# Sending the last four tiles' rows from the sync engine in a gated cross-attention and ternary FFN block, with another order of the end

## The chip, the cores and the metric

The kernel runs on one core of a Trainium2 chip. Its time is device microseconds of one execution; the median of several executions is given. The engines are named as in the profile: PE (TensorE), DVE (VectorE), ACT (ScalarE), POOL (GpSimd) and SP (the sync engine, which here only starts transfers).

## What is computed

For 16 batches of 224 rows of 512 numbers, a Flamingo-like block: attention of the normalised rows to a masked context, added to the rows with a gate, and then a feed-forward layer whose weights are rounded to -1, 0 or 1 and whose activations are rounded to 8 bits, added with a second gate. Cut to what matters here:

```python
def act_quant(x):
    scale = 127.0 / clip(max(abs(x), axis=-1), 1e-05)
    return clip(round(x * scale), -128.0, 127.0) / scale

def bitlinear(x, w, b):                     # w: ternary after weight_quant
    return einsum('bsd,fd->bsf', act_quant(rmsnorm(x)), weight_quant(w)) + b

def ffn(x, w1, b1, w2, b2):                 # 512 -> 2048 -> 512
    return bitlinear(gelu(bitlinear(x, w1, b1)), w2, b2)

x = x + tanh(g_xattn) * attention(layernorm(x), ctx, mask)
x = x + tanh(g_ffn) * ffn(layernorm(x), w1, b1, w2, b2)
```

## The kernel before

**Order of the rows.** The masks leave a different number of context rows in each batch, so the kernel sorts the batches by that number and treats them in that order. The 3584 rows make 28 tiles of 128 rows; seven tiles hold four batches, so a tile can hold the end of one batch and the start of the next. The table `sh.token` holds for each place in a tile the number of its row in memory, computed on the chip. Rows are fetched (`fetch_x`) and the results sent (`store`) by indirect transfers that POOL starts and that read their row numbers from this table.

**Pairs.** The feed-forward part treats the tiles in 14 pairs (`NPAIR`); tile (i, k) is tile 2i + k. A tile goes through `residual` (fetch), `project` (the attention's output projection, added on DVE at line 1255), `normalise` (the rounding to 8 bits; the result `xq` is turned by a transposing transfer from SP, or, in the last pair, by PE in `turn_rows`), `up` (w1 on PE, eviction to `h` on DVE), `gelu`, `down` (w2 on PE) and `store`.

`gelu` applies the function on ACT, takes the largest absolute value on DVE (line 1369), scales to 16-bit integers in the tile `hq` (line 1372), casts these to bf16 (line 1375 on DVE; line 1379 in two halves on ACT for pair 12), and has `hq` turned into `hqT`: by a transposing transfer from SP, or for tile (12, 1) by PE in `turn_by_tensor`, whose result ACT copies (line 1355). ACT also sums the squares, and POOL makes of them and of the maximum the factor `c2` (lines 1272 to 1274).

**The last pair** has its own functions, since nothing lies behind it to fill the engines. `up_last` works in halves of 1024 columns: eviction (DVE, line 1419), gelu (ACT, line 1422), maximum of the half (DVE, line 1423). `gelu_last` takes the maximum of the two (line 1434), and scales and casts each half (lines 1441 and 1442). `mean_square` sums the squares on ACT, `measure_last` makes `c2` on POOL. `turn_by_tensor` turns `hq` on PE.

**Who orders the work.** The framework puts each engine's instructions in an order by the program's text and its own reckoning of what is ready, and adds the semaphores. `tc.issue_after(x)` asks that what is traced in its block stands behind `x` on the engine of `x`. Each engine then runs its instructions strictly in that order. At the end of the program, written out by hand, the calls are:

```python
    mean_square(i, 1)
    added, sent = store(i - 1, 1)
    gelu_last(i, 0)
    with tc.issue_after(added):
        gelu_last(i, 1)
    with tc.issue_after(raised):
        turn_by_tensor(i, 0)
    with tc.issue_after(sent):
        measure_last(i, 0)
        measured = measure_last(i, 1)
```

with i = 13. `store` adds the product to the rows on DVE (line 1485) and sends them from POOL (line 1487). The whole compact path stands in a branch on `n_odd` (line 250 loads it into every engine's registers); line 1826 is the end of the program, where SP waits for every transfer and each engine drains and meets the others.

Of the kernel before, what the change touches and what calls it, by code (L numbers as in the profile page):

```python
# [734 lines left out]
def compact_path(ctx, tc, sh, x, context, out, late_loads, stages):  # L735
# [541 lines left out]
    def normalise(i, ks=(0, 1)):  # L1277
        f = pairs[i]
        y = f["y"]
        name = f"{i}_{ks[0]}"  # L1280
        part = slice(ks[0], ks[-1] + 1)
        mv = small(f"mv_y{name}", 4).rearrange("p (k n) -> p k n", k=2)
        if ks[0] == 0:
            f["fx"] = late["rows"].tile([P, 2, D], F32, tag="hq", name=f"fx_{i}", bufs=3)
            f["xq"] = pa.tile([P, 2, D], BF16, tag="xq", name=f"xq_{i}", bufs=3)
            f["xqT"] = pa.tile([P, 2 * ND, P], BF16, tag="xq", name=f"xqT_{i}", bufs=3)
        fx, xq, xqT = f["fx"], f["xq"], f["xqT"]
        for k in ks:
            st = small(f"bs_y{name}_{k}", 6)
            nc.vector.bn_stats(st, y[:, k, :])  # L1290
            nc.vector.bn_aggr(mv[:, k, :], st)
            nc.vector.tensor_scalar(fx[:, k, :], y[:, k, :], mv[:, k, 0:1], None, ALU.subtract)  # L1292
        amax = small(f"a1_{name}")
        nc.vector.tensor_reduce(amax[:, part], fx[:, part, :], AX.X, ALU.max, apply_absolute_value=True)

        scale = quantiser(amax, part, 1e-5 * EPS, f"1_{name}")

        for k in ks:
            nc.vector.tensor_scalar(xq.bitcast(I16)[:, k, :], fx[:, k, :], scale[:, k : k + 1], None, ALU.mult)
        rounded = nc.vector.tensor_copy(xq[:, part, :], xq.bitcast(I16)[:, part, :])  # L1300
        if i < NPAIR - 1:
            nc.sync.dma_start_transpose(
                out=xqT[:, ks[0] * ND : (ks[-1] + 1) * ND, :], in_=xq[:, part, :].rearrange("p n d -> p (n d)")
            )

        r = small(f"r1_{name}")
        nc.gpsimd.tensor_scalar(r[:, part], mv[:, part, 1], 1.0 + EPS, EPS * EPS, ALU.mult, ALU.add)
        pow_half(r[:, part])
        c = unquantiser(amax, r, part, sh.isw[0], f"1_{name}")
        for k in ks:  # L1310
            f["c1", k] = c[:, k : k + 1]
            nc.gpsimd.tensor_tensor(y[:, k, :], y[:, k, :], sh.b2, ALU.add)  # L1312
        load["v"] += len(ks) * (850 + 340 + 667 + 450 + 220)
        return rounded.ins
# [43 lines left out]
    def gelu(i, ks=(0, 1)):  # L1358
        f = pairs[i]
        name = f"{i}_{ks[0]}"  # L1360
        part = slice(ks[0], ks[-1] + 1)
        ss = small(f"ss_{name}")
        amax = small(f"a2_{name}")
        for k in ks:
            if (i, k) != (NPAIR - 2, 1):
                nc.scalar.activation(f["h", k], f["h", k], AF.Gelu)  # L1366
        for k in ks:
            h = f["h", k]
            nc.vector.tensor_reduce(amax[:, k : k + 1], h, AX.X, ALU.max, apply_absolute_value=True)  # L1369
            scale = quantiser(amax, slice(k, k + 1), 1e-5 * EPS**0.5, f"2_{i}_{k}")  # L1370
            hq = late["rows"].tile([P, FF], BF16, tag="hq", name=f"hq_{i}_{k}", bufs=3)
            nc.vector.tensor_scalar(hq.bitcast(I16), h, scale[:, k : k + 1], None, ALU.mult)  # L1372
            f["hqT", k] = hqT = late["rows"].tile([P, NF, P], BF16, tag="hqT", name=f"hqT_{i}_{k}", bufs=2)
            if i < NPAIR - 2:
                late["rounded"] = nc.vector.tensor_copy(hq, hq.bitcast(I16)).ins
            else:
                for g in range(2):
                    cols = slice(g * FF // 2, (g + 1) * FF // 2)
                    nc.scalar.copy(hq[:, cols], hq.bitcast(I16)[:, cols])
            f["hq", k] = hq  # L1380
            if (i, k) != (NPAIR - 2, 1):
                nc.sync.dma_start_transpose(out=hqT, in_=hq)
        if (i, ks[0]) == (NPAIR - 2, 1):
            f["a2", 1] = amax[:, 1:2]
            return
        for k in ks:
            nc.scalar.activation(f["h", k], f["h", k], AF.Square, accum_out=ss[:, k : k + 1])  # L1387
        r = small(f"r2_{name}")
        nc.gpsimd.tensor_scalar(r[:, part], ss[:, part], 1.0 / FF, EPS, ALU.mult, ALU.add)
        pow_half(r[:, part])  # L1390
        c = unquantiser(amax, r, part, sh.isw[1], f"2_{name}")
        for k in ks:
            f["c2", k] = c[:, k : k + 1]
        load["v"] += len(ks) * (2282 + 1280 + 690)
        load["s"] += len(ks) * 2 * 1910 + 2600

    def up_last(i, k):

        f = pairs[i]
        if k == 0:  # L1400
            place = pa.tile([P, 12, S], F32, tag="pT", name="h_last", bufs=1)
            h = place.rearrange("p n q -> p (n q)")[:, :FF]
        else:
            h = xoT.rearrange("p n q -> p (n q)")[:, :FF]
        most = small(f"am_{i}_{k}")
        for g in range(2):
            ph = wide([P, 2, NB], F32, f"hp_{i}_{k}_{g}")
            for n in range(2):
                at = (2 * g + n) * NB
                for d in range(ND):  # L1410
                    last = nc.tensor.matmul(
                        ph[:, n, :],
                        lhsT=f["xqT"][:, k * ND + d, :],
                        rhs=w1T[:, d, at : at + NB],
                        start=(d == 0),
                        stop=(d == ND - 1),
                    )
            cols = slice(2 * g * NB, 2 * (g + 1) * NB)
            nc.vector.scalar_tensor_tensor(
                h[:, cols], ph.rearrange("t i n -> t (i n)"), f["c1", k], sh.b1[:, cols], ALU.mult, ALU.add  # L1420
            )
            nc.scalar.activation(h[:, cols], h[:, cols], AF.Gelu)
            nc.vector.tensor_reduce(most[:, g : g + 1], h[:, cols], AX.X, ALU.max, apply_absolute_value=True)
        f["h", k], f["most", k] = h, most
        return last.ins

    def gelu_last(i, k):

        f = pairs[i]
        name = f"{i}_{k}"  # L1430
        part = slice(k, k + 1)
        h = f["h", k]
        amax = small(f"a2_{name}")
        nc.vector.tensor_reduce(amax[:, part], f["most", k], AX.X, ALU.max)
        scale = quantiser(amax, part, 1e-5 * EPS**0.5, f"2_{name}")
        hq = late["rows"].tile([P, FF], BF16, tag="hq", name=f"hq_{name}", bufs=3)
        f["hqT", k] = hqT = late["rows"].tile([P, NF, P], BF16, tag="hqT", name=f"hqT_{name}", bufs=2)
        half = FF // 2
        for g in range(2):
            cols = slice(g * half, (g + 1) * half)  # L1440
            nc.vector.tensor_scalar(hq.bitcast(I16)[:, cols], h[:, cols], scale[:, part], None, ALU.mult)
            nc.vector.tensor_copy(hq[:, cols], hq.bitcast(I16)[:, cols])
        f["hq", k], f["a2", k] = hq, amax[:, part]

    def mean_square(i, k):
        f = pairs[i]
# [15 lines left out]
    def measure_last(i, k):  # L1462
        f = pairs[i]
        c = unquantiser(f["a2", k], f["r2", k], slice(0, 1), sh.isw[1], f"2_{i}_{k}")
        f["c2", k] = c[:, 0:1]
        return latest["p"]
# [14 lines left out]
    def store(i, k):  # L1481
        f = pairs[i]
        po = f["po", k]
        y = f["y"][:, k, :]
        added = nc.vector.scalar_tensor_tensor(y, po, f["c2", k], y, ALU.mult, ALU.add)  # L1485
        load["v"] += 700
        sent = nc.gpsimd.indirect_dma_start(  # L1487
            out=out_rows,
            out_offset=bass.IndirectOffsetOnAxis(ap=token(2 * i + k), axis=0),
            in_=y,  # L1490
            in_offset=None,
            bounds_check=B * S - 1,
            oob_is_err=False,
        )
        return added.ins, sent.ins

    NPAIR = NTOK // 2

# [212 lines left out]
    for s in range(B):  # L1711
# [33 lines left out]
        if s + 1 < B:  # L1745
            scores(s + 1, 0)
            scores(s + 1, 1)

    i = NPAIR - 1
    residual(i)  # L1750
    with tc.issue_after(late["av"]), tc.issue_after(late["rounded"]):
# [27 lines left out]
        turn_by_tensor(i - 1, 1)  # L1779
        lowered = down(i - 1, 1)  # L1780
    mean_square(i, 1)
    added, sent = store(i - 1, 1)
    gelu_last(i, 0)
    with tc.issue_after(added):
        gelu_last(i, 1)
    with tc.issue_after(raised):
        turn_by_tensor(i, 0)
    with tc.issue_after(sent):
        measure_last(i, 0)
        measured = measure_last(i, 1)  # L1790
    with tc.issue_after(lowered):
        down(i, 0, lambda: turn_by_tensor(i, 1))
    with tc.issue_after(measured):
        store(i, 0)
    down(i, 1)
    store(i, 1)

# [33 lines left out]
```

## Time and profile before

| | |
|---|---|
| median of 3 runs | 740.0 us (739.37 to 740.6) |
| the profiled execution: its time | 735.04 us |
| its span, first to last instruction | 733.0 us |
| mean granted PE clock | 0.981 |
| PE busy | 676.0 us (92%) |
| DVE busy | 492.2 us (67%) |
| ACT busy | 416.2 us (57%) |
| POOL busy | 394.1 us (54%) |
| indirect sends of results, POOL | 28 |
| transposing transfers, SP | 25 of `hq`, 14 of `xq` |

The profile is of one execution. Busy shares are over the whole span; the change concerns the last 60 us, so the shares say little of it, and the lines of that stretch are read instead. In lines of the timeline the first column is the start and the second the length, in us from the start of the span; in brackets stands how long the engine was idle before, and what ended this. "PEq", "SPq" and so on are an engine's sequencer, which waits, branches, drains or starts transfers. Lines of the source are those of the kernel before.

### The profile page before, as it was taken

The numbers are of one execution on the slowest core, as the hardware profiler recorded it, in microseconds if no ns is written. First come the engines' busy times: TensorE is split into PE (matmuls) and PEld (weight loads), VectorE is DVE, ScalarE is ACT, GpSimd is POOL, SyncE is SP. The second block draws the span as 40 slices with busy tenths as digits, with TensorE's granted clock in tenths as the row PEclk, the third lists the DMA queues.
The fourth block names the chain that finished last, engine by engine and source line by source line (L and its number), as shares of the span: only waits on it lengthen the run. The fifth ranks groups of instructions, "written<-read, shape, count | busy, mean of one in ns | idle before, by whom it ended". The sixth has DMA issues, their size and how long they took to land.

```text
span 733.0 us, 11422 instructions
## 1 busy us (share of the span) xinstructions
PE 676.0 (92%) x3917; PEld 432.1 (59%) x3917; DVE 492.2 (67%) x1294; ACT 416.2 (57%) x978; POOL 394.1 (54%) x549
## 2 busy tenths in 40 slices
PE   4998899999999999897999999999999999999862
PEld 3876677666555656564556665766665665544331
DVE  5586856877484775673667857839585765889760
ACT  2549555384673864646627549547373746574560
POOL 5583676464464644755447562656545453554631
PEclk9989999999999999999999999999999999999997
DMA  7884031032222232321233321123313221422200
GB/s 236 288 288 144 14 104 32 16 75 57 65 54 58 83 58 72 70 59 58 54 61 104 58 81 38 41 72 74 83 43 72 58 59 44 86 73 58 58 15 33
DMA packets 79858, 56.74 MB, mean 77 GB/s; under 512 B 68176, under 2 KB 68320, under 8 KB 79664
## 3 DMA queue, kind: packets, MB, share of 16 engines
q1 hardware_dynamic: 71728, 30.17, 17.6%
q0 software_dynamic: 8064, 25.76, 11.4%
q8 instruction: 33, 0.54, 0.3%
q14 instruction: 33, 0.27, 0.1%
HBM read 32.06 MB, written 7.34 MB: 54 GB/s over the span
## 4 chain that ended last, share of the span: by engine, by line
PE 63%; DVE 10%; issue 9%; POOL 9%; ACT 4%; DMA 3%; POOLq 0%; DVEq 0%; ACTq 0%
PE qp L1066 11%; PE op L1252 10%; PE fp L1472 8%; PE hp L1333 8%; PE kp L946 5%; PE sim L1106 4%; PE vp L962 4%; PE ptp L1163 3%; PE av L1188 2%; POOL p L1140 2%; DVE a L1369 2%; PE xnp L1045 2%; POOL x L808 2%; DMA hqT<-hq 1%; POOL out_dram L1487 1%
## 5 line engine op out<-in xcount | busy, mean ns | idle before, releaser
L1140 POOL TENSOR_TENSOR p<-p,rec 112x768 f32<-112x768 f32 (+2 forms) x64 | 79.6, 1246 | 72.0 <-DVE rec L1139 28.1
L1130 ACT ACTIVATE p<-p,nm 112x192 f32<-112x192 f32 (+2 forms) x256 | 104.8, 413 | 10.3 <-DVE nm L1120 7.3
L1472 PE MATMUL fp<-w2T,hqT 128*128 128x512 fp8e4 x448 | 102.6, 382 | 3.8 <-DMA hqT<-hq 2.2
L1066 PE MATMUL qp<-xnT,wq_sb 128*128 128x224 f32 x512 | 105.1, 359 | 0.6 <-ACT xnT L781 0.6
L1252 PE MATMUL op<-wo_sb,xoT 128*128 128x512 f32 x224 | 103.7, 599 | 0.0
L1333 PE MATMUL hp<-w1T,xqT 128*128 128x512 fp8e4 x416 | 99.3, 383 | 3.0 <-DVE nm L1120 1.4
L1066 PEld LDWEIGHTS qp<-xnT,wq_sb 128*128 128x128 f32 x512 | 97.0, 193 | 6.4 <-issue 3.1
L1341 DVE SCALAR_TENSOR_TENSOR h<-hp,c,b_bc 128x1024 f32<-128x1024 f32 x52 | 66.5, 1281 | 43.6 <-PE hp L1333 43.3
L1120 DVE CUSTOM_DVE_ANT_0 p<-sim,mask 112x192 f32<-112x192 f32 (+2 forms) x224 | 56.0, 303 | 32.5 <-PE sim L1106 31.9
L1472 PEld LDWEIGHTS <-hqT 128*128 128x128 bf16 x448 | 42.7, 98 | 58.8 <-issue 6.3
L1369 DVE TENSOR_REDUCE a<-h 128x1 f32<-128x2048 f32 x26 | 59.3, 2281 | 20.3 <-ACT h L1366 20.3
L1487 POOL DMA_INDIRECT out_dram<-y,token x28 | 32.0, 1143 | 67.2 <-DVE y L1485 62.1
L1333 PEld LDWEIGHTS <-xqT 128*128 128x128 bf16 x416 | 39.9, 98 | 47.4 <-issue 8.5
L1485 DVE SCALAR_TENSOR_TENSOR y<-fp,c,y 128x512 f32<-128x512 f32 x28 | 20.9, 746 | 68.0 <-PE fp L1472 66.4
L1252 PEld LDWEIGHTS op<-wo_sb,xoT 128*128 128x128 f32 x224 | 40.7, 190 | 38.8 <-issue 36.3
L946 PE MATMUL kp<-ctxT,wk_sb 128*128 128x192 f32 (+1 forms) x360 | 59.9, 316 | 0.0
L946 PEld LDWEIGHTS kp<-ctxT,wk_sb 128*128 128x128 f32 x360 | 54.5, 198 | 5.4 <-issue 3.8
L1387 ACT ACTIVATE h<-h 128x2048 f32<-128x2048 f32 x25 | 47.7, 1909 | 17.1 <-DVE hq L1372 11.8
L1312 POOL TENSOR_TENSOR y<-y,b_bc 128x512 f32<-128x512 f32 x28 | 37.0, 1321 | 34.6 <-DVE fx L1292 34.3
L781 ACT COPY pT<-ptp 128x448 f32<-128x448 f32 (+1 forms) x62 | 32.3, 536 | 39.9 <-PE ptp L1163 39.7
L781 ACT COPY qT<-qp 128x448 f32<-128x448 f32 x29 | 15.4, 532 | 65.7 <-PE qp L1066 65.4
L1106 PE MATMUL sim<-kT,qT 64*112 64x192 f32 (+2 forms) x512 | 50.8, 311 | 0.6 <-DVE nm L1120 0.6
(200 smaller groups left out, 1250.5 us busy)
## 6 DMA issues: line engine op xcount, KB each, us to landing
raw<-in_L_ffn_w_dram SPq DMA_DIRECT2D x16, 512.0 KB, 5.4
wq_sb<-in_L_xattn_W_q_dram SPq DMA_DIRECT2D x1, 1024.0 KB, 5.8
b_bc<-in_L_ffn_b_dram SPq DMA_DIRECT2D x1, 1024.0 KB, 8.3
wk_sb<-in_L_xattn_W_k_dram SPq DMA_DIRECT2D x1, 768.0 KB, 7.4
wv_sb<-in_L_xattn_W_v_dram SPq DMA_DIRECT2D x1, 768.0 KB, 8.8
wo_sb<-in_L_xattn_W_o_dram SPq DMA_DIRECT2D x1, 512.0 KB, 4.0
wo_sb<-in_L_xattn_W_o_dram SPq DMA_DIRECT2D x2, 256.0 KB, 6.0
y<-in_x_dram,token POOLq DMA_INDIRECT x28, 3.5
```

The costliest lines, as they stand in the source:

```text
L946: nc.tensor.matmul(pk[:, p - p0, :], lhsT=sh.wk[:, c, p * P : (p + 1) * P], rhs=st["ctxT"][:, c, :cap], start=(c == 0), stop=(c == NC - 1),)
L1066: nc.tensor.matmul(pq[:, i, :], lhsT=sh.wq[:, d, (p + i) * P : (p + i + 1) * P], rhs=st["xnT"][:, d, :], start=(d == 0), stop=(d == ND - 1),)
L1106: nc.tensor.matmul(sim[:, j, i, :cap], lhsT=st["qT"][j * DH : (j + 1) * DH, p, q * TQ : (q + 1) * TQ], rhs=keys["kT"][j * DH : (j + 1) * D ...
L1120: nc.vector.tensor_tensor_reduce(out=probs[:, h, :cap], in0=sim[:, j, i, :cap], in1=keys["mask"][:, first + j * begin : first + j * begin ...
L1130: nc.scalar.activation(probs[:, h, :cap], probs[:, h, :cap], AF.Exp, bias=nmax, scale=-1.0, accum_out=total[:TQ, h : h + 1],)
L1140: nc.gpsimd.tensor_tensor(probs[:, :, first : first + cap], probs[:, :, :cap], rec[:TQ].unsqueeze(2).to_broadcast([TQ, 4, cap]), ALU.mult,)
L1252: last = nc.tensor.matmul(po, lhsT=xoT[:, d, at : at + P], rhs=sh.wo[:, d, :], start=(d == 0), stop=(d == ND - 1))
L1333: last = nc.tensor.matmul(ph[:, n, :], lhsT=f["xqT"][:, k * ND + d, :], rhs=w1T[:, d, at : at + NB], start=(d == 0), stop=(d == ND - 1),)
L1341: nc.vector.scalar_tensor_tensor(h[:, cols], ph.rearrange("t i n -> t (i n)"), f["c1", k], sh.b1[:, cols], ALU.mult, ALU.add)
L1369: nc.vector.tensor_reduce(amax[:, k : k + 1], h, AX.X, ALU.max, apply_absolute_value=True)
L1387: nc.scalar.activation(f["h", k], f["h", k], AF.Square, accum_out=ss[:, k : k + 1])
L1472: last = nc.tensor.matmul(po, lhsT=f["hqT", k][:, n, :], rhs=w2T[:, n, :], start=(n == 0), stop=(n == NF - 1))
```

## The change

- `store` for pairs 12 and 13 (the last four tiles) no longer uses POOL. SP sends the rows with plain transfers, to row numbers that it holds in registers. Since a tile can hold rows of two batches, each of which is one run of rows in memory, tiles (12, 0) and (13, 0) are sent in two pieces (64 and 64 rows; 32 and 96), the others in one: six transfers.
- SP loads three row numbers from `sh.token` into registers, behind the transposing transfer of `xq` of pair 8. The others follow by adding constants.
- In `gelu`, the cast for pair 12 is done on DVE, in one piece, as for the other pairs, in place of ACT in two halves; SP's transposing transfer for (12, 0) and PE's transposing for (12, 1) depend on it.
- In `up_last`, the maxima of the halves stand behind the cast of tile (12, 1) on DVE.
- At the end, the add of tile (12, 1) on DVE stands behind `gelu_last(13, 0)` instead of before it, and `measure_last` and the last two stores are no longer held behind POOL's sends.

```diff
         if i < NPAIR - 1:
-            nc.sync.dma_start_transpose(
+            pairs[i]["turning"] = nc.sync.dma_start_transpose(
...
-            if i < NPAIR - 2:
-                late["rounded"] = nc.vector.tensor_copy(hq, hq.bitcast(I16)).ins
-            else:
-                for g in range(2):
-                    cols = slice(g * FF // 2, (g + 1) * FF // 2)
-                    nc.scalar.copy(hq[:, cols], hq.bitcast(I16)[:, cols])
+            late["rounded"] = nc.vector.tensor_copy(hq, hq.bitcast(I16)).ins
...
-            nc.vector.tensor_reduce(most[:, g : g + 1], h[:, cols], AX.X, ALU.max, apply_absolute_value=True)
+            with tc.issue_after(late["rounded"]):
+                nc.vector.tensor_reduce(most[:, g : g + 1], h[:, cols], AX.X, ALU.max, apply_absolute_value=True)
...
-            nc.vector.tensor_copy(hq[:, cols], hq.bitcast(I16)[:, cols])
+            rounded = nc.vector.tensor_copy(hq[:, cols], hq.bitcast(I16)[:, cols])
         f["hq", k], f["a2", k] = hq, amax[:, part]
+        return rounded.ins
...
         added = nc.vector.scalar_tensor_tensor(y, po, f["c2", k], y, ALU.mult, ALU.add)
         load["v"] += 700
-        sent = nc.gpsimd.indirect_dma_start(
+        if i >= NPAIR - 2:
+            for p, n, at in late["pieces"][2 * i + k]:
+                nc.sync.dma_start(out_rows[bass.ds(at, n), :], y[p : p + n, :])
+            return added.ins
+        nc.gpsimd.indirect_dma_start(
...
+    with tc.issue_after(pairs[NPAIR - 6]["turning"].ins):
+        where = [
+            nc.values_load(
+                sh.token[p : p + 1, t // 7, t % 7 : t % 7 + 1],
+                engines=[mybir.EngineType.SP],
+                min_val=0,
+                max_val=B * S - n,
+            )
+            for p, t, n in ((0, NTOK - 4, 64), (64, NTOK - 4, S), (32, NTOK - 2, S))
+        ]
+
+    late["pieces"] = {
+        NTOK - 4: [(0, 64, where[0]), (64, 64, where[1])],
+        NTOK - 3: [(0, 128, where[1] + 64)],
+        NTOK - 2: [(0, 32, where[1] + 192), (32, 96, where[2])],
+        NTOK - 1: [(0, 128, where[2] + 96)],
+    }
...
-    added, sent = store(i - 1, 1)
-    gelu_last(i, 0)
+    with tc.issue_after(gelu_last(i, 0)):
+        added = store(i - 1, 1)
     with tc.issue_after(added):
         gelu_last(i, 1)
     with tc.issue_after(raised):
         turn_by_tensor(i, 0)
-    with tc.issue_after(sent):
-        measure_last(i, 0)
-        measured = measure_last(i, 1)
+    measure_last(i, 0)
+    measure_last(i, 1)
     with tc.issue_after(lowered):
         down(i, 0, lambda: turn_by_tensor(i, 1))
-    with tc.issue_after(measured):
-        store(i, 0)
+    store(i, 0)
```

More of the change, by code (lines that the diff above doesn't have):

```diff
@@ L1494, in store @@
         )
-        return added.ins, sent.ins
     NPAIR = NTOK // 2
```

## The prediction

> **What bounds the kernel now.** The diff touches only the end, so after the page (TensorE 92% busy over the whole span) I read the end: first line 1826, where the program closes, in the stretch from 721 to 725 us of the 733.0 us span. Columns: count, shortest/median/longest in ns, first and last start.
>
> ```profile
> L1826 SPq EVENT_SEMAPHORE  x11: 28/28/41362, 682.3 to 724.2; - x11
> L1826 SPq DRAIN  x2: 7/10/13, 724.3 to 724.4; - x2
> L1826 DVEq DRAIN  x1: 57/57/57, 722.4 to 722.4; - x1
> L1826 POOLq DRAIN  x1: 8887/8887/8887, 723.3 to 723.3; - x1
> ```
>
> SP has seen every transfer land and is ready to close at 724.4, VectorE at 722.4. POOL (GpSimd) starts a drain at 723.3 that takes 8.9 us, to 732.2; the closing exchange of semaphores takes the remaining 0.8 us. So for 7.8 us (724.4 to 732.2) only POOL's drain holds the program. The chain of work that ended last does not say so: it stops at POOL's last send.
>
> ```profile
> 717.08 2.81 DMA out_dram<-y,token
> 719.89 0.03 issue
> 719.91 0.02 POOLq L1487
> ...
> 720.66 0.97 POOL out_dram L1487
> ```
>
> Here the last send's queue first waits until the send before it has landed (719.89): sends to the output are kept in series, because their rows are not known when the program is made. Next the timeline of all engines, 700 us to the end, and ScalarE's from 674 to 706:
>
> ```profile
> 705.37 0.75 DVE L1485 SCALAR_TENSOR_TENSOR y<-fp,c,y 128x512 f32<-128x512 f32 x1 [1.71 <-PE fp L1472]
> ...
> 707.94 0.96 DVE L1442 CAST hq<-hq 128x1024 bf16<-128x1024 int16 x2
> ...
> 708.63 1.48 PE L1354 MATMUL hqp<-ident,hq 128*128 128x128 bf16 x16 [3.36 <-DVE hq L1442]
> ...
> 714.04 5.34 PE L1472 MATMUL fp<-w2T,hqT 128*128 128x512 fp8e4 x24
> ...
> 719.49 0.75 DVE L1485 SCALAR_TENSOR_TENSOR y<-fp,c,y 128x512 f32<-128x512 f32 x1 [2.71 <-PE fp L1472]
> ```
>
> ```profile
> 677.61 1.98 ACT L1379 CAST hq<-hq 128x1024 bf16<-128x1024 int16 x2
> ...
> 697.63 1.98 ACT L1379 CAST hq<-hq 128x1024 bf16<-128x1024 int16 x2
> ```
>
> VectorE idles 1.71 us for the down product of tile (12,1), adds it, and only then quantises tile (13,0); TensorE meanwhile idles 3.36 us. The two casts of pair 12 hold ScalarE 2 us each, on the way to the transposes. Last, the sizes of transfers (KB where fixed, median us to landing):
>
> ```profile
> out_dram<-y,token POOLq DMA_INDIRECT x28, 2.9
> ...
> m<-in_mask_BxS_bk_dram SPq DMA_DIRECT2D x1, 11.7 KB, 1.8
> ```
>
> **The change part by part.** All against that execution (span 733.0, its time 735.04); the median shown is 740.0, 5 us more than the profiled one, and I carry the difference of spans over to it unchanged.
>
> Step 1, POOL's drain leaves the end. POOL's last indirect send becomes that of tile (11,1), at 678.2 now. What the drain waits for the trace does not say. Lower bound: it waits for the software-made sends; from the last such send to the drain's end are 732.2 - 720.7 = 11.5 us, so it would be over by 690 and cost nothing. Upper bound: it always takes 8.9 us once POOL has nothing left. POOL's last work is then the scale c of tile (13,1), about 708 by step 4; the drain now starts 2.9 us after POOL's last branch (720.43), so 708 + 2.9 + 8.9 = 719.8, about where SP is ready (step 5: 720.2). In both cases SP sets the end. **-7.8 us.** A rule of the Trainium skill speaks against this: "VectorE: DVE Perf Modes", section The DRAIN you can't avoid, holds the drains of the program's frame to be boilerplate, constant at about 12 ns on all five engines. By it there is nothing to win here, and the sum would be 4.0 us (step 4) instead of 11.8. This case's row has 8,887 ns, with SP's and VectorE's at 7 to 57; I follow the row.
>
> Step 2, the two casts of pair 12 move to VectorE: 2 x 1.98 us off ScalarE, 2 x 0.69 onto VectorE (L1375, 2048 columns). Tile (12,0): scaled at 677.28, cast on VectorE by 678.0 (678.6 if the add of tile (11,1) goes between; that add, and its send, then shift 0.7 and nobody waits). The transposing DMA, 4.57 us from issue to landing, then lands at 682.6 to 683.2 instead of 684.2. TensorE is busy with the output projection to 683.14, so its down product starts about 1.0 earlier and no more. But the next step, transposing tile (13,0)'s xq, waits for VectorE's cast at 687.05, which hangs on that projection and doesn't move: of 1.0 us remain 0.6 at the up product of (13,0) and, through VectorE's eviction, 0.85 at that of (13,1), which ends at 696.1.
>
> Step 3, tile (12,1): the maxima of h_last (2 x 1.2 us) are now behind its cast. VectorE: reduction to 691.2, two evictions woven in to 693.7, scale 1.29, cast 0.69: 695.7 instead of ScalarE's 699.6. TensorE transposes as soon as the up product ends, 696.1; ScalarE copies 2 x 0.99, its squares being over at 696.8; the down product runs 697.9 to 701.6 instead of 701.5 to 705.3. 3.7 us gained on TensorE.
>
> Step 4, who is late next: VectorE. From 693.7 it has in line: scale and cast 2.0, maxima of (13,0) 2.4, evictions of (13,1) 2.5, maxima of (13,1) 2.4, quantising (13,0) 2.8, the add of (12,1) 0.75, quantising (13,1) 2.8: 15.6 us, no idling in it, so 709.3 instead of 711.1. Quantising (13,0) is now ahead of the add, so the add's wait for TensorE holds up only (13,1), and by then the product is there. TensorE: transposes (13,0) at about 703.5 to 705.5, first half of its down product to about 707.5, then a wait for the first half cast of (13,1), 708.6; transposes to 709.9, second half 1.85, down product of (13,1) 3.65: 715.4 instead of 719.4. **-4.0 us**, between -1.8 (VectorE's own gain) and -5. The granted clock was 0.57 from 708.6 to 712.6, behind TensorE's idling; shorter idling may spare about 1 us of this, which the lower bound holds.
>
> Step 5, the sends. SP is idle from 681.7, so issuing six pieces of some 0.4 us hides behind its own waiting. Its reaction is short: the cast at 661.68 is followed by the transposing DMA at 661.71. No row has a plain SP write to memory. From below: the mask's 1.8 us; from above: an indirect send, 3.0 for the last. The loads of w1 land 512 KB every 1.35 us, so 256 KB add 0.7: an estimate of 2.45 for a whole tile, 1.95 for 32 rows, 2.25 for 96. If the pieces stay in series, tile (13,0) takes 0.03 + 1.95 + 0.06 + 2.25 = 4.3 us, while the next add ends 3.45 after it: the last send leaves 0.85 late. Add to landing: 0.85 + 0.03 + 2.45 = 3.3, against 723.64 - 720.24 = 3.4 now. **0 us**, between -0.9 (not in series) and +1.2. The upper end is by the skill's "DMA: Bandwidth & Descriptors", section Anatomy of one DMA (about 2.0 us fixed per DMA, plus bytes over 436 GB/s, which speaks against splitting a tile): 2.15 + 2.45 + 2.6. By the trace's rows the split costs 0.85, by the rule 1.2; I take the rows. Behind it SP needs the same 0.7 us of waits and the 0.8 of closing: 716.2 (step 4: 715.4 and the 0.75 add) + 3.3 + 0.7 = 720.2, end 721.0 to 721.2.
>
> Step 6, loading three row numbers to SP: the load of n_odd took SP 0.9 us with its check, so 2.7 in all, after the turning of pair 8. SP waits 5 to 25 us between transposing DMAs there: hidden, at worst 2.7 once. **0 us.** The waits around measure_last go: POOL's scales no longer stand behind a send, and nobody waited for them.
>
> Sum: 7.8 + 4.0 + 0 + 0 = 11.8 us; span 721.2, time 740.0 - 11.8 = **728.2**.
>
> **The rivals.** (a) VectorE becomes the bound, or its order is woven other than I think (an eviction between scale and cast, the maxima of (13,1) ahead of quantising (13,0)): the end keeps only 0.5 to 2.5 of the 4.0 us. For it: 15.6 us of queued work and a gain there of only 1.8. Time 729.7 to 731.7, say 730.7. (b) The drain follows the landing of any transfer: it ended 8.6 us after the last one. Then 716.2 + 3.3 + 8.6 + 0.8 = 728.9, time 735.9. Against: SP's sends are not POOL's business; no row shows it. (c) Slower: the sends in series become the bound. From the add of (13,0) (712.8) three pieces follow one another, then 1.5 us of closing: the gain is gone when a piece takes (733.0 - 1.5 - 712.8) / 3 = 6.2 us; at 8.3, the longest SP transfer of the trace (1 MB), time 746. Against: 256 KB took SP 4.5 beside other loads, and nothing else moves here.
>
> **How the numbers follow.** My forecast 0.60, (a) 0.27, (b) 0.08, (c) 0.05. The range 725.0 to 731.5 holds the forecast with its bounds (sends not in series -0.9, order -1, clock -1; +1.2) and most of (a), and leaves out (b) and (c). Faster by over 0.2% (1.5 us, about what can be told from no change): the first three, 0.95; of (c) 0.02 lies within it and 0.03 beyond.
>
> **What would show it.** Right: no drain of POOL's in the last 5 us before the close, SP's the last to arrive; the cast of (12,1) on VectorE near 695.7; its down product from about 698; the last add ending near 716; last landing 3.3 after it. Wrong: POOL's drain still ending last; the last add after 719; pieces that take over 4 us.

## The result, and the profile after

| | before | after |
|---|---|---|
| median of 6 runs | 740.3 us (739.37 to 743.31) | 728.47 us (724.51 to 730.5) |
| ratio, 95% interval | | 0.9833 (0.9803 to 0.9862) |
| profiled execution: time, span | 735.04, 733.0 us | 730.5, 728.4 us |

The change is worth 11.8 us, 1.7%. The two spans differ by only 4.6 us, because the profiled execution of after reached the end late and that of before early. So the ends are compared from one event that the change does not touch, the start of POOL's send of tile (11,0): 666.10 us before, 670.47 after (665.6 to 671.0 in the traces of all the large kernels here). In numbers that start at this event ("in the tail", from here on) the program ends at 66.93 before and at 57.93 after: 9.0 us earlier.

First the closing line of the program after, from 716 us to the end; columns: count, shortest/median/longest in ns, first and last start.

```profile
L1842 POOLq DRAIN  x3: 45/107/8561, 716.4 to 728.1; - x3
L1842 SPq DRAIN  x3: 7/7/13, 727.5 to 727.8; - x3
...
L1842 DVEq DRAIN  x2: 10/34/58, 724.3 to 727.9; - x2
```

POOL's long drain has not gone. It takes 8.56 us, as before, but it starts at 716.4, when POOL has no work left, and is over at 725.0. SP is ready 2.6 us after that, at 727.6, and sets the end. Next the timeline of all engines after (start, length, engine, line, operation; in brackets the idle time before it and what ended it), for the steps that the prediction took in turn:

```profile
680.37 1.29 DVE L1372 TENSOR_SCALAR hq<-h,k 128x2048 int16<-128x2048 f32 x1
681.57 0.74 DVE L1482 SCALAR_TENSOR_TENSOR y<-fp,c,y 128x512 f32<-128x512 f32 x1
...
682.60 1.28 POOL L1488 DMA_INDIRECT out_dram<-y,token  x1 [7.18 <-DVE y L1482]
682.98 2.11 SPq L1377 DMA_TRANSPOSE hqT<-hq  x1
...
689.76 1.90 PE L1469 MATMUL fp<-w2T,hqT 128*128 128x512 fp8e4 x8 [2.26 <-DMA hqT<-hq]
...
700.62 1.28 DVE L1414 SCALAR_TENSOR_TENSOR xoT<-hp,c,b_bc 128x1024 f32<-128x1024 f32 x1
701.81 0.69 DVE L1374 CAST hq<-hq 128x2048 bf16<-128x2048 int16 x1
...
702.89 1.04 ACT L1448 ACTIVATE sq<-h_last 128x1024 f32<-128x1024 f32 x1
...
703.93 1.04 ACT L1448 ACTIVATE sq<-h_last 128x1024 f32<-128x1024 f32 x1
...
704.97 1.90 ACT L1355 COPY hqT<-hqp 128x1024 bf16<-128x1024 bf16 x2
...
706.02 5.31 PE L1469 MATMUL fp<-w2T,hqT 128*128 128x512 fp8e4 x16 [2.39 <-ACT hqT L1355]
...
717.73 0.75 DVE L1482 SCALAR_TENSOR_TENSOR y<-fp,c,y 128x512 f32<-128x512 f32 x1 [2.85 <-PE fp L1469]
721.18 0.75 DVE L1482 SCALAR_TENSOR_TENSOR y<-fp,c,y 128x512 f32<-128x512 f32 x1 [2.71 <-PE fp L1469]
```

The same steps of tiles (12,0) and (12,1) before:

```profile
678.23 1.10 POOL L1487 DMA_INDIRECT out_dram<-y,token  x1 [7.19 <-DVE y L1485]
...
679.61 2.04 SPq L1382 DMA_TRANSPOSE hqT<-hq  x1
...
684.23 3.63 PE L1472 MATMUL fp<-w2T,hqT 128*128 128x512 fp8e4 x16 [1.09 <-DMA hqT<-hq]
...
701.51 3.75 PE L1472 MATMUL fp<-w2T,hqT 128*128 128x512 fp8e4 x16 [1.23 <-ACT hqT L1355]
```

Four things are to be seen. With the cast on VectorE, SP's transposing transfer of (12,0) (682.98) starts 0.4 us behind POOL's send of (11,1) (682.60) instead of 1.4, and TensorE waits 2.26 us for it instead of 1.09. The cast of (12,1) stands behind an eviction (700.62). ScalarE's two squares of `h_last` stand ahead of its copies of `hqT`. And the down product of (12,1) takes 5.31 us instead of 3.75. The last add ends at 721.93, 51.46 in the tail; before it was 54.14. Why the down product is long shows in the busy table by stretches (length; busy us of PE, PEld, DVE, ACT, POOL; granted clock; DMA share; GB/s):

```profile
701.00:706.00 5.00, 1.79 (x20) 1.01 (x18) 5.00 (x6) 4.07 (x7) 0.68 (x3) 1.00 0.00 0
706.10:709.50 3.40, 3.40 (x9) 1.24 (x10) 2.53 (x5) 3.40 (x5) 0.17 (x1) 0.50 0.00 0
709.60:716.00 6.40, 5.70 (x50) 3.32 (x49) 5.18 (x12) 2.74 (x5) 4.08 (x9) 1.00 0.13 45
```

For 3.4 us the granted clock is 0.50, with 1.00 on both sides. TensorE had been busy for 1.79 of the 5.00 us ahead of it. Last, SP's sends:

```profile
L1486 SPq DMA_DIRECT2D out_dram<-y x6: 320/364/582, 694.5 to 724.6; - x6
```

The last of the six sends is issued at 724.6, 2.7 us after its add. From the last add to SP ready it takes 5.65 us; with POOL's send it took 4.13. The 9.0 us of the tail are thus 7.8 of the drain, plus 2.7 of the last add, minus 1.5 of the sends.

### The profile page after: what moved, and what is told of

It is laid out like the page before. It is cut to its first block, busy times and chain, and to the rows that moved or that the text cites. A ratio compares the mean times of both kernels' runs of the same rounds, so it can differ in the third digit from the quotient of the medians.

```text
span 728.4 us, 11444 instructions
## 1 busy us (share of the span) xinstructions
PE 677.1 (93%) x3917; PEld 432.7 (59%) x3917; DVE 495.1 (68%) x1296; ACT 413.0 (57%) x974; POOL 389.3 (53%) x545
## 4 chain that ended last, share of the span: by engine, by line
PE 70%; DVE 10%; issue 6%; POOL 6%; DMA 3%; ACT 3%; POOLq 0%; DVEq 0%; ACTq 0%
PE op L1252 11%; PE qp L1066 11%; PE fp L1469 11%; PE hp L1333 9%; PE kp L946 6%; PE sim L1106 5%; PE vp L962 5%; PE ptp L1163 3%; PE av L1188 3%; POOL p L1140 2%; DMA hqT<-hq 2%; POOL x L808 2%; PE xnp L1045 1%; DVE a L1369 1%; PE ctxp L935 1%
## 5 line engine op out<-in xcount | busy, mean ns | idle before, releaser
L1488 POOL DMA_INDIRECT out_dram<-y,token x24 | 27.6, 1148 | 57.9 <-DVE y L1482 53.6
```

## The experiments

Spans from one profile, times as medians with their ratio to the kernel before on the same chip. Tail numbers are counted from POOL's send of (11,0), as above.

**The sends alone, and the order alone.** `sends_only` is the kernel before with SP's pieces and their row numbers; casts and order stay. `order_only` is the changed kernel with POOL's sends. In both, `measure_last` and the last stores no longer stand behind POOL's sends.

```diff
# sends_only, against before
+        if i >= NPAIR - 2:
+            for p, n, at in late["pieces"][2 * i + k]:
+                nc.sync.dma_start(out_rows[bass.ds(at, n), :], y[p : p + n, :])
+            return added.ins
# order_only, against after
-        if i >= NPAIR - 2:
-            for p, n, at in late["pieces"][2 * i + k]:
-                nc.sync.dma_start(out_rows[bass.ds(at, n), :], y[p : p + n, :])
-            return added.ins
```

> The kernel before with only the sends of the last four tiles moved to SP (and the three row numbers loaded); the order of the engines' work and the casts on ScalarE stay. Counted from POOL's send of tile (11,0), the last add ends 54.1 us later in the kernel before and its span ends 66.9 later. Theory 1 (the end is held by POOL's drain of 8.6 to 8.9 us, which starts when POOL has nothing left, so taking the last sends from POOL is what pays, whatever the order): the last add stays at 54 to 55, SP is ready about 5 later, the end comes at 60 to 61, 6 to 7 us earlier than before, about 733.5 us. Rival (the order of the end is what pays): no more than 1 to 2 us, 738 to 740 us.

> The changed kernel with all sends still from POOL; only the new order of the end and the casts on VectorE. Theory 1: the last add comes 2.7 us earlier, as in the changed kernel, POOL's drain still follows the last send and ends last: end 64 to 65 us after the send of tile (11,0), some 2.6 us below before, about 737.5 us. Rival (the order is what pays): 730 us or less.

Measured: `sends_only` 733.11 us, ratio 0.991 (0.9883 to 0.9937); `order_only` 735.7 us, ratio 0.9955 (0.9939 to 0.997). The closing lines of `sends_only` and then of `order_only`:

```profile
L1844 POOLq DRAIN  x3: 45/107/8560, 716.2 to 732.2; - x3
L1844 SPq DRAIN  x3: 7/7/13, 731.6 to 731.9; - x3
```

```profile
L1822 POOLq DRAIN  x3: 45/107/8887, 725.5 to 735.0; - x3
L1822 SPq DRAIN  x3: 7/7/13, 726.3 to 734.7; - x3
```

In `sends_only` the drain runs from 716.2 to 724.8 and SP is ready at 731.7; in `order_only` SP is ready at 726.4 and the drain runs on to 734.4. In the tail the sends alone bring 4.45 us: 7.8 of the drain, minus 1.4 for the later landing, minus 2.0 because the last add comes later than the expected 54 to 55, at 56.13: this trace has two stretches at half clock in the tail, one on the down product of (12,1) and one on that of (13,0), where before has one. The order alone brings 2.74, which is the last add. So the bigger part of the gain is the drain, and each part brings something without the other. Their sum is 7.2 of the 9.0 us. What is missing is about the size of that late add of `sends_only`; whether its order brings the second slow stretch every time, one profile does not show.

**POOL kept to the end.** `pool_late` is the changed kernel with one small operation of POOL behind the last add, whose result nobody reads:

```diff
     store(i, 1)
+    nc.gpsimd.tensor_tensor(sh.mhalf[:, 0:1], pairs[i]["y"][:, 1, 0:1], sh.mhalf[:, 1:2], ALU.add)
```

> The changed kernel with one more POOL instruction, an addition of one column that reads the result of the last add and is used by nothing. Theory 1 (the drain takes 8.6 to 8.9 us from the end of POOL's last work, whatever that was): POOL ends some 10.5 us after the last add, 62 us after the send of tile (11,0), and the end moves about 5 us later than in the changed kernel, to about 733.5 us. Rival (the drain waits for software-made sends, the last of which is 40 us back, or for POOL's pile of earlier work): the end stays, 728.5 us.

Measured: 735.28 us, ratio 0.994 (0.9917 to 0.9963). The closing line:

```profile
L1843 POOLq DRAIN  x3: 45/107/8560, 724.6 to 733.7; - x3
L1843 SPq DRAIN  x3: 7/7/13, 727.5 to 733.4; - x3
```

One operation of 0.19 us takes back 5.95 us of the 9.0 in the tail (6.8 of the 11.8 by the medians). The drain is again 8.56 us, though POOL's last indirect send lies 42 us back, and it starts 2.8 us after this new last operation. It follows neither the software-made sends nor the last landing, but POOL's own last work.

**What the drain's length hangs on.** Three programs that compute nothing of the reference: some VectorE copies, plain sends of the output, and one tile of input that is fetched by SP (`drain_plain`), by one indirect transfer of POOL (`drain_indirect`), or by 40 of them (`drain_forty`).

```diff
-    nc.sync.dma_start(y, x_rows[0:P, :])
+    for n in range(40):                    # drain_indirect: once, into y
+        nc.gpsimd.indirect_dma_start(out=w[:, n % 4, :], in_=x_rows, ...)
```

> A small program by itself, which computes nothing of the reference: SP fetches 128 rows, POOL makes row numbers and doubles the rows, VectorE copies them twenty times, SP writes 28 tiles; POOL has no indirect transfer and is done long before the end. It measures POOL's drain alone. If the drain is the price of having used software-made transfers: well under 1 us here, and 8.6 us with one indirect fetch. If it is POOL's whatever it did: 8.6 us here too.

> The same small program with the fetch made by one indirect transfer of POOL instead of SP's plain one, over 20 us before the end. Price of having used software-made transfers at all: a drain of about 8.6 us. Price of each transfer (24 in the changed kernel, 28 in the kernel before, for 8.56 and 8.89 us): under 1 us. POOL's whatever it did: 8.6 us, as without.

> The small program with forty indirect fetches instead of one; nothing of the reference is computed. The drains of eight profiles are 83 ns for each of POOL's indirect transfers in the whole program: 8.89 us with 107, 8.56 with 103, 8.48 with 102; and the drain with one fetch outlasted POOL's last work by 0.09 us more than without any. Theory (83 ns per transfer, however long ago): the drain ends 3.3 to 3.4 us after POOL's last work. Rival (a fixed price in a large program, and the count a coincidence): 0.2 us.

Measured: 37.98, 40.02 and 91.21 us, one run each; the times matter less than the closing drains of the three, in this order:

```profile
L61 POOLq DRAIN  x3: 34/76/1599, 3.3 to 35.9; - x3
```

```profile
L68 POOLq DRAIN  x3: 34/101/1704, 5.2 to 38.0; - x3
```

```profile
L70 POOLq DRAIN  x3: 40/101/4898, 56.4 to 89.2; - x3
```

Here the drain is issued while POOL's one operation (1.5 us) still runs, so the row holds that too. Past the operation's end it lasts 0.07, 0.16 and 3.36 us with 0, 1 and 40 transfers: (3.36 - 0.07) / 40 = 82 ns each. The large kernel agrees. Its indirect transfers are these groups of POOL after (columns: count | busy us, mean ns | idle before):

```profile
L808 POOL DMA_INDIRECT y<-in_x_dram,token x28 | 29.0, 1036 | 29.5 <-DMA out_dram<-y,token 22.3 <-issue 3.8 <-DVE w L1595 2.7
L808 POOL DMA_INDIRECT x<-in_x_dram,token x26 | 28.5, 1095 | 7.5 <-issue 6.3 <-PE ctxp L935 0.4 <-PE qp L1066 0.3
L1488 POOL DMA_INDIRECT out_dram<-y,token x24 | 27.6, 1148 | 57.9 <-DVE y L1482 53.6 <-issue 1.8 <-DVE k L1265 1.0
L908 POOL DMA_INDIRECT ctx<-in_ctx_dram,keys x21 | 23.6, 1122 | 13.5 <-DVE y L1255 9.5 <-issue 2.4 <-DVE ind L846 0.3
L808 POOL DMA_INDIRECT xoT<-in_x_dram,token x2 | 2.3, 1149 | 1.1 <-DVE xoT L887 0.8 <-issue 0.3
L908 POOL DMA_INDIRECT xoT<-in_ctx_dram,keys x2 | 2.0, 978 | 0.6 <-DVE ind L846 0.3 <-issue 0.3
```

They are 28 + 26 + 24 + 21 + 2 + 2 = 103, and 8,561 / 103 = 83.1 ns. Before, with 28 sends, they are 107, and 8,887 / 107 = 83.1. The three kernels below with 102 show 8,478 or 8,479: 83.1 again. The drain is a price of 83 ns per indirect transfer of the whole program, paid once, when POOL is finished. All these transfers take 128 row numbers, so whether the price goes by transfer or by row is not shown.

**One piece for tile (13,0).** `one_piece` sends this tile in one transfer to consecutive rows, so its first 32 rows go to a wrong place.

```diff
-        NTOK - 2: [(0, 32, where[1] + 192), (32, 96, where[2])],
+        NTOK - 2: [(0, 128, where[1] + 96)],
```

> The changed kernel with tile (13,0) sent in one piece of 128 rows instead of 32 and 96 (its first 32 rows go to the wrong place). Theory (the sends are in series, and the split holds up the last send: 2.7 us in the profile of the changed kernel, of which 1.7 are one engine's time for a fetch of program code): the last send leaves within 0.1 us of the last add and SP is ready 3.2 us after the add; then POOL's drain ends last, and the end is 2 to 2.7 us earlier than in the changed kernel, about 726 us. Rival (the sends are hidden behind the drain or the closing anyway): no change, 728.5 us.

Measured: 727.07 us, ratio 0.983 (0.9798 to 0.9862). SP's sends, then the closing line:

```profile
L1486 SPq DMA_DIRECT2D out_dram<-y x5: 332/379/573, 691.2 to 719.7; - x5
```

```profile
L1842 POOLq DRAIN  x3: 45/107/8561, 714.1 to 723.3; - x3
L1842 SPq DRAIN  x3: 7/7/13, 722.3 to 723.0; - x3
```

The last send goes out at 719.7, 0.03 us behind its add, and SP is ready 2.7 us after that add instead of 5.65. But the drain of POOL (714.1 to 722.7) now outlasts SP, and the last add came 2.6 us later in this run (54.02 in the tail, two down products at half clock), so the program ends at 57.91 in the tail, as after; the expected gain of 2 us or more did not come, and the ratio is that of the change. The delay of the sends is shown; that it costs 3 us of total time is not, since the next bound lies close behind.

Where the delay comes from: in the trace's packets of after, 90 of the 96 rows of the second piece moved from 721.46 to 722.44. The other 6, one in 16, moved one behind the other from 723.19 to 724.04, directly behind a 16 KB packet of the instruction queue, 721.61 to 723.21, which began 0.4 us after VectorE's branch behind the last add. This fits one of the 16 DMA engines being held up by a fetch of code; the trace does not name the engine of a packet. That piece took 3.6 to 4.1 us from issue to the next issue in `after`, `sends_only`, `pool_late`, a repeat of after and `send_behind` (below), and in each its last 6 rows began within 0.02 us of the end of such a fetch; the pieces of 32 and 64 rows, for which the next one waited too, took 2.1 to 2.6. In `planned3` below the same fetch hit another send: 8 of the last tile's rows moved from 716.87 to 717.88, behind a fetch from 715.13 to 716.89; the other 120 were through at 716.15. The coincidence is plain; no kernel took the fetch itself away.

**The two transfers apart.** `send_behind` is the changed kernel with the send of tile (11,1) on SP too, behind the transposing transfer of (12,0):

```diff
-        if i >= NPAIR - 2:
+        if i >= NPAIR - 2 or (i, k) == (NPAIR - 3, 1):
...
-    store(i - 2, 1)
+    with tc.issue_after(late["turned"]):
+        store(i - 2, 1)
```

> The changed kernel with the send of tile (11,1) also from SP, queued behind the transposing transfer of hqT of tile (12,0). In the changed kernel POOL's send of that tile starts 0.4 us before this transfer, and the transfer lands 6.8 us after its issue instead of 4.6, so that TensorE waits 2.3 us for it. Theory (the two transfers hinder each other): the transfer lands after 4.5 us, the down product of (12,0) starts at 17.1 after the send of tile (11,0) instead of 19.3, and the last add comes 1.5 to 2.2 us earlier (49.5 to 50), end about 56, time about 726.5 us. Rival (the transfer takes longer for another reason, or VectorE holds the end anyway): hqT still 6.8 us, or the last add still at 51.5, 728.5 us.

Measured: 726.88 us, ratio 0.9839 (0.9817 to 0.9862). Its timeline:

```profile
681.74 1.96 SPq L1377 DMA_TRANSPOSE hqT<-hq  x1
684.12 0.56 SPq L1486 DMA_DIRECT2D out_dram<-y  x1
...
686.12 1.90 PE L1469 MATMUL fp<-w2T,hqT 128*128 128x512 fp8e4 x8
```

No bracket stands behind the down product of (12,0): TensorE did not wait for the transfer. It starts 4.4 us after the transfer's issue, where it started 6.8 after it with the two together. In the tail this product ends at 20.73 instead of 23.14, the last add at 49.76 instead of 51.46, the program at 55.95 instead of 57.93. The ratio alone could not tell it from the change; the trace can.

**The order as the prediction had it.** `planned2` is `send_behind` with what the prediction took for granted written out: the cast of (12,1) directly behind its scale, the squares behind the copies of `hqT`, the maxima of (13,1) behind the quantising of (13,0). It also departs from the prediction in one place: TensorE runs the down product of (13,0) in one piece, ahead of the transposes of (13,1), where the change puts these between its halves. `planned3` moves the squares of (13,1) too, and makes the factor `c2` of the last pair on VectorE, so that POOL is done earlier. `planned2_again` is `planned2` once more, and `after_again` the changed kernel, on the chip of `planned3`.

```diff
# planned2, against send_behind (cut)
+            with tc.issue_after(late["rounded"]) if k else ExitStack():
                 ...                      # evictions of (13, 1)
-        mean_square(i, 0)
+    with tc.issue_after(turned):         # turned = turn_by_tensor(i - 1, 1)
+        mean_square(i, 0)
...
+    with tc.issue_after(rounded):        # rounded = gelu_last(i, 0)
+        greatest = maxima(i, 1)
+    with tc.issue_after(greatest):
         added = store(i - 1, 1)
...
-        down(i, 0, lambda: turn_by_tensor(i, 1))
+        lowered = down(i, 0)
+    with tc.issue_after(lowered):
+        turn_by_tensor(i, 1)
# planned3, against planned2
-    mean_square(i, 1)
+    with tc.issue_after(turned):         # turned = turn_by_tensor(i, 0)
+        mean_square(i, 1)
...
+            nc.vector.tensor_tensor(c[:, 0:1], f["a2", k], f["r2", k][:, 0:1], ALU.mult)
+            nc.vector.tensor_scalar(c[:, 0:1], c[:, 0:1], 1e-5, sh.isw[1], ALU.max, ALU.mult)
```

> The version that the readings ask for: the former edit, and the evictions of tile (13,1) behind the cast of (12,1); ScalarE's squares of (13,0) behind the copies of hqT of (12,1); VectorE quantises (13,0) before it takes the maxima of (13,1); TensorE runs the down product of (13,0) in one piece, so that its add and its two sends come well before the last ones. Expected: cast of (12,1) at 29, down product of (12,1) from 31, last add at 48 to 49; the last send no longer waits for the pieces before it, SP ready 2.7 to 3.2 us after the last add, POOL's drain over at about 52, end at 52 to 53.5 after the send of tile (11,0): 4.5 to 6 us below the changed kernel, 723 to 724 us. Rival (VectorE's total of work sets the end whatever the order): last add at 50 or later, 726 us or more.

> The version planned2 once more, to compare it with the changed kernel on one chip: its end came 3.4 us earlier than the changed kernel's, counted from the send of tile (11,0), with a down product of (13,0) that ran 1.6 us longer at the lower clock. Expected 2 to 4 us below the changed kernel, 724 to 726.5 us.

> planned2 with ScalarE's squares of (13,1) behind the copies of hqT of (13,0), and the scales c of pair 13 made by VectorE instead of POOL, so that POOL is done sooner. In planned2 the copies wait until 707.5 for the squares though the transposes are done at 706.3. Theory: down product of (13,0) from 37.8 instead of 39.0 and at full clock, last add at 47.7 to 49, SP ready 3.4 us later, POOL's drain over by 52.5 and perhaps last: end 52.5 to 54, 0.5 to 2 us below planned2. Rival (POOL's drain ends last, because the squares of (13,1) and with them POOL's last work come later): 54.5 or more, no gain.

> The changed kernel once more, unaltered, beside the two versions of this call. In its first profile the piece of 96 rows of tile (13,0) took 3.9 us, the other pieces 2.1 to 2.4; six of its packets stood behind a fetch of 16 KB of program code that started 0.4 us after VectorE's last branch. Theory (the fetch comes with the branch, so it meets this piece every time): again 3.6 to 4.0 us, the last send 2.2 to 2.7 us behind the last add, end 57 to 58 after the send of tile (11,0). Rival (a chance meeting): 2.2 us, and an end nearer 56. Time 727 to 729 us by both.

| | time, us | ratio to before |
|---|---|---|
| `planned2` | 726.2 (724.52 to 726.38) | 0.9829 (0.9806 to 0.9853) |
| `planned2_again` | 725.24 (723.15 to 727.42) | 0.9808 (0.9781 to 0.9835) |
| `planned3` | 723.01 (722.18 to 723.54) | 0.9784 (0.9764 to 0.9805) |
| `after_again` | 728.5 (727.38 to 728.71) | 0.9859 (0.9835 to 0.9882) |

`planned3` beats both kernels; from the changed one, on the same chip, it is 5.5 us away and the intervals do not meet. Timeline of `planned2` at tile (12,1):

```profile
696.80 1.29 DVE L1372 TENSOR_SCALAR hq<-h,k 128x2048 int16<-128x2048 f32 x1
698.12 0.69 DVE L1374 CAST hq<-hq 128x2048 bf16<-128x2048 int16 x1
...
699.59 1.93 ACT L1355 COPY hqT<-hqp 128x1024 bf16<-128x1024 bf16 x2 [1.81 <-PE hqp L1354]
...
700.66 3.63 PE L1480 MATMUL fp<-w2T,hqT 128*128 128x512 fp8e4 x16 [0.66 <-ACT hqT L1355]
...
708.53 5.27 PE L1480 MATMUL fp<-w2T,hqT 128*128 128x512 fp8e4 x16 [1.72 <-ACT hqT L1355]
```

With scale, cast and copies in line the down product of (12,1) starts at 31.13 in the tail and takes 3.63 us. The next one, of (13,0), took the slow stretch instead: 5.27 us, behind copies that stood behind squares. So `planned2` missed what was expected of it: with its last add at 50.31 and 726.2 us it landed where its rival, VectorE's total of work, had put it. `planned3` puts those squares away too, and there both run at full speed. Its timeline, and its closing line:

```profile
697.70 3.63 PE L1485 MATMUL fp<-w2T,hqT 128*128 128x512 fp8e4 x16 [0.66 <-ACT hqT L1355]
...
704.52 3.63 PE L1485 MATMUL fp<-w2T,hqT 128*128 128x512 fp8e4 x16 [0.66 <-ACT hqT L1355]
...
713.67 0.75 DVE L1498 SCALAR_TENSOR_TENSOR y<-fp,c,y 128x512 f32<-128x512 f32 x1 [3.72 <-PE fp L1485]
```

```profile
L1868 POOLq DRAIN  x3: 45/107/8478, 710.9 to 719.9; - x3
L1868 SPq DRAIN  x3: 7/7/13, 718.8 to 719.6; - x3
```

The last add ends at 47.85 in the tail, 6.3 us earlier than before the change, though VectorE has four operations more to do than in `planned2`, and it waits 3.72 us for TensorE: the rival of `planned2` is refuted. The drain ends last again (710.9 + 8.5 = 719.4, SP at 718.8): the program is back at the bound from which it started, with 0.5 us between the two.

## Why the prediction was right, and where it was not

The forecast was 728.2 us and the measured time is 728.47. Its largest term was right for the right reason. Steps 2, 3 and 5 failed, and what they cost was made good by a gain that the tail does not explain: that the two numbers agree so closely is luck.

- **Step 1, the drain: right, 7.8 us.** Of its two bounds the upper one holds: `pool_late` shows that the drain comes in full once POOL has nothing left, and the small programs what it is made of. The prediction had the drain start 2.9 us after POOL's last branch and end at 719.8, 53.7 in the tail; measured 2.75 and 54.50. The rule of the Trainium skill that it set aside ("VectorE: DVE Perf Modes", The DRAIN you can't avoid: about 12 ns on every engine) fails for POOL here by 8.5 us; SP's and VectorE's rows, 7 to 58 ns, are nearer to it.
- **Step 2, the casts of pair 12: failed.** Instead of 1.0 us gained at the down product of (12,0), 1.2 were lost at its start. The cast itself came as forecast (over at 12.44 in the tail; 678.6 is 12.5), with the add of (11,1) between scale and cast. What failed is the 4.57 us from issue to landing, which the prediction kept for a transfer that it issued 1 us earlier. The send of (11,1) did not shift (12.13 in the tail in both kernels); the transposing transfer moved up to it, and "nobody waits" was wrong: its reader started 6.8 us after its issue instead of 4.6. In the packets of before, the send took 0.97 us and the transposition behind it 2.63; after, both lie mixed over 4.9 us. With them apart (`send_behind`) the product starts 1.25 earlier than before, as step 2 had it. A hint was in the trace of before: sends to the output took 2.9 us to landing in the median, but 6.1 at most.
- **Step 3, tile (12,1): the mechanism right, the order not.** The cast ended at 32.03 in the tail, not 29.6 (an eviction between scale and cast, and the late start from step 2), ScalarE's squares stood ahead of the copies though the prediction had them "over at 696.8", and the half-clock stretch fell on the product: end at 40.86 where 35.5 was worked out. So 3.7 us of gain became 1.7 of loss. Written out in `planned2` the cast ends at 29.29 and the product at 34.76: the arithmetic holds when the order does.
- **Step 4, the last add: 2.7 us instead of 4.0,** inside its bounds of 1.8 to 5. It survived the failure of step 3 because the quantising of (13,0) no longer waits for the add of (12,1), as step 4 said: the down product of (13,0) starts 1.6 us earlier (42.63 in the tail against 44.26). The other 1.05 us are its length, 4.52 us instead of 5.57. The clock's slow stretch was not spared; it moved off this product, from 709.11 to 712.52 before to 706.13 to 709.54 after, 3.41 us long in both, onto that of (12,1), whose delay no longer held up the quantising. The prediction had about 1 us for the clock, but from shorter idling. Its list for VectorE names the maxima of (13,1) ahead of the quantising of (13,0), while its rival (a) and its times for TensorE put them behind; they came ahead.
- **Step 5, the sends: 1.5 us lost instead of none,** beyond its upper bound of 1.2. The 0.85 of waiting was foreseen; the missing term is some 1.7 us for the 96-row piece, put at 2.25 and measured at 4.0, whose last rows came behind a fetch of code. The rule from which the prediction had its upper bound (the Trainium skill, "DMA: Bandwidth & Descriptors", Anatomy of one DMA) is fitted there to transfers that GpSimd issues. SP's last pieces of 32 and 128 rows had their last packet 1.6 and 1.8 us after the issue, where the rule gives 2.15 and 2.6.
- **Step 6: right.** The three loads take 524.90 to 527.27, 2.4 us, and SP then waits 18.8 for its next work.

Of the rivals, (a) described the order that came ("an eviction between scale and cast, the maxima of (13,1) ahead of quantising (13,0)"; these start at 705.86 and 707.86, it at 709.57), and the last add's 2.7 us lies just above its 0.5 to 2.5. (b) is refuted: after the change the drain ended 2.6 us before SP was ready. (c) did not decide: the piece of 4.0 us stayed under its 6.2. (Its 8.3 us is not the longest SP transfer of the trace: one of 768 KB took 8.8.)

Of the signs of being right, SP did arrive last, but POOL's drain ended 3.4 us before the end, inside the 5 us that were to be free of it; the cast and the down product of (12,1) came 2.4 and 3.7 us later than named and the last add 1.6, and the last packet landed 4.5 us after it instead of 3.3. Of the signs of being wrong, one stood at its edge: a piece of over 4 us (4.0 here, 4.06 in `after_again`).

The tails add up to 9.0 us, the medians differ by 11.8, with an interval of 10.2 to 14.6 (ratio times 740.3). All tails are set against the one profiled execution of before, 735.04, which lay 5 us under its median; over the ten timed comparisons the medians' gain exceeds the tail's by 1.7 us on average (-0.4 to 3.2). Whether the typical end of before is longer than the profiled one, or the part ahead of the tail shorter after, one profile of before can't say. It stays open, and the agreement within 0.3 us rests on it: by the tail alone the time would have been about 731.

## What to carry to other kernels

At the end of a program, list when each engine drains and for how long: an engine with a long drain must get its last work early, and one small operation placed late on it gives most of the gain back. When a cast, send or add is moved "and nobody waits", look which transfers then start together. An order that a forecast relies on has to be written into the program; here writing it out, with the two transfers kept apart, was worth about 3 us more (`planned2`, 725.24 against 728.5 us on one chip, the intervals just touching), and 5.5 with the further moves of `planned3`.

## What the runs showed of the hardware

- POOL's closing drain costs 83 ns for each indirect transfer (of 128 rows) in the whole program (8.89 us at 107, 8.56 at 103, 8.48 at 102; 3.3 at 40), with the last one up to 42 us back (`pool_late`).
- A transposing transfer of 512 KB let its reader start 6.8 us after the issue when an indirect send of 256 KB ran in the midst of it; alone, within 4.4.
- A 16 KB packet of code took 0.9 to 1.8 us (three such in the last 22 us of each large program). In six traces one in 16 of the rows of a send that was then under way began just as it ended, and came up to 1.7 us behind the others.
- A plain send of SP in pieces of 32 or 64 rows took 1.75 to 2.6 us from its issue to the next, when the next was waiting.
- The stretch at half clock in the tail was 3.41 us long in both kernels. The down products of 3.6 us that it met took 5.0 to 5.3.
